# Attention's own rows by block load instead of gather, and VectorE's steps of two interleaved streams held in written order

## The chip, the cores and the metric

The kernel is one program on one core of a Trainium2 chip. Its time is device microseconds, the median of three runs. TensorE (PE) multiplies, VectorE (DVE) and ScalarE (ACT) do elementwise work and reductions, GpSimd (POOL) here mostly writes the descriptors of indirect DMAs (gathers and scatters by a list of row numbers), and SyncE (SP) issues plain DMAs. Each engine works through its own instruction queue in order and waits at an instruction until its inputs are there.

## The reference

Four graph layers run one after another on x, 8 batches of 2048 nodes with 64 features, each of the form x = x + layer(relu(layernorm(x))). The change lies where the third layer (index 2) ends and in the fourth (index 3). Cut to these:

```python
# third layer, three steps; its last step gives v, and x = x + v
effects = einsum('nm,bmd->bnd', adj, v)
v = relu(concat([v, effects]) @ W1.T + b1) @ W2.T + b2
# fourth layer: attention over all 2048 nodes
h = x @ weight                       # 8 batches x 64 = 512 numbers a node
e = leaky_relu((h @ a[:64])[:, :, None] + (h @ a[64:])[:, None, :], 0.2)
e = adj * e                          # adj holds 0 and 1: no edge gives e = 0, not minus infinity
out = softmax(e) @ h + bias
```

Since a missing edge counts with exp(0 - top) and not with zero, the kernel takes the sum of h over all nodes once (`total`), scaled by exp(-top), and corrects it for the few neighbours that each node has.

## The kernel before, in words

**The fourth layer's tiles.** Nodes are ranked by degree; the 16 tiles of 128 nodes are tiles of ranks, not of node numbers. `order` holds, for tile t, the 128 node numbers of its ranks (`order[:, 1, t]`, the gather list) and, the other way round, the ranks of the 128 nodes of node tile t (`order[:, 0, t]`). Tile 0, the nodes of highest degree, is done densely (`Near.first_tile`). Tiles 1 to 15 are done from lists of neighbours (`Near.others`), in the order `TILES = [15, 13, 11, 1, 10, 2, 9, 3, 8, 4, 7, 5, 6, 12, 14]`.

**What a tile needs.** In the third layer's last step `Scores.chunk` makes h for every node tile (512 numbers a node, kept in SBUF as `rows(t)`) and 16 scores a node, and SP writes both to a DRAM table `f_rows` (528 numbers a row, L2899 and L2900). `Near.block(t)` then fills n = NEAR[t] + 1 places of a ring of 36 with indirect DMAs from `f_rows` that POOL issues (L2966): place 0 is the tile's own rows, by `order`, the others its neighbours, by `near`. The first two blocks are asked for ahead of everything, and block `place + 2` at the end of the tile at `place`.

**A sparse tile's work** (L2998 to L3052). The opening: L3011 adds the tile's own score to the neighbours' scores (it reads all n places, so it waits for all of them), then L3015 to L3028 are small DVE and ACT steps that make the weights `e`, `none` and `den`. The body: DVE multiplies rows by weights into `y` (L3056 for one row, L3037 for two; y has four places), and PE adds each of the n + 1 results to `acc` in PSUM by a product with the identity matrix. The close: DVE writes `o` = `acc` x `den` (L3056), and one tile later POOL scatters `o` to `att_rows` (L2977).

**The dense tile's work** (`first_tile`, L3061 to L3146). It gathers 128 rows of adj (L3067) and its own rows `mine`, makes scores, and then takes 16 steps, one for each source tile jt: 16 exponentials on ACT (L3119, L3120), `tensor_max` (L3123) and `tensor_mul` (L3124) on DVE, and 8 products of 128x65 and one of 128x512 (`plain`) on PE. Its `m` has two buffers for each of two terms, so the exponentials of step jt wait for the products of step jt - 2.

**How the two are woven.** Both are generators. `layer3_near` (L2067) takes the first piece of each, then 12 more pieces of `first_tile` (up to and with the `tensor_mul` of jt = 2), then one piece of `first_tile` after each piece of `others`. This is the written order. It isn't the issue order: a planner ahead of the run sorts each engine's instructions by its own estimates of when inputs will be there, keeping what the data need. `kern.behind(x)` (L193) ties x, in issue order alone, behind the instruction written just before it on the same engine. It is used before in `Lists.fill`, and nowhere in the fourth layer.

**The third layer's end.** In its last step the same weaving has `Feed` gather rows `raw` for PE (L2636, POOL), while `advance` takes pieces of `chunk` for groups of 4, 4, 4, 2 and 2 node tiles (L2864 to L2901). `order` is a tile of this layer, written by `neighbours` and stored to DRAM (`order3`); the fourth layer loads it back.

**The end.** After all scatters SP loads `att_rows` back (L3152), PE transposes it, DVE adds x, and ACT issues the stores (L3148 to L3167).

Of the kernel before, what the change touches and what calls it, by code (L numbers as in the profile page):

```python
# [7 lines left out]
F = mybir.dt.float32  # L8
# [3 lines left out]
I32 = mybir.dt.int32  # L12
AF = mybir.ActivationFunctionType
OP = mybir.AluOpType
# [5 lines left out]
P = 128  # L20
NB = 8
N = 2048
D = 64
# [112 lines left out]
class Kernel:  # L136
# [8 lines left out]
    def __init__(self, tc, ctx, a):  # L145
        self.tc, self.nc, self.a = tc, tc.nc, a
        self.flip = 0
        self.short = False
        self.consts = ctx.enter_context(tc.tile_pool(reuse_waits="tile", name="consts", bufs=1))

        dram = ctx.enter_context(tc.tile_pool(reuse_waits="tile", name="dram", bufs=1, space=bass.MemoryType.DRAM))
        self.xs = [
            [a["xT"][:, :, c * CW : (c + 1) * CW].rearrange("q p n -> p q n") for c in range(NC)]
        ]


        self.h_rows = dram.tile([N, ROW], F, name="h_rows")
        self.g_rows = dram.tile([N, NB * D], F, name="g_rows")
        self.order3 = dram.tile([P, 2, NT], I32, name="order3")

        self.links = dram.tile([N, N], BF, name="links")
        self.sent = [dram.tile([N, NB * D], F, name=f"sent{i}") for i in range(5)]


        self.f_rows = dram.tile([N, WIDE], F, name="f_rows")
        self.att_rows = dram.tile([N, NB * D], F, name="att_rows")
        self.rdeg = dram.tile([NT, P], F, name="rdeg")

        self.h_sums = [dram.tile([8, P, CW], F, name=f"sums{q}") for q in range(NP)]
        self.h_parts = [dram.tile([P, 3, N], BF, name=f"parts{q}") for q in range(NP)]  # L170
        for i in range(3):
            self.xs.append([dram.tile([P, NP, CW], F, name=f"x{i}_{c}") for c in range(NC)])
        self.setup()
# [1841 lines left out]
    def neighbours(self, k, bank, slots):  # L2015

        nc = self.nc
        order = k.tile([P, 2, NT], I32, name="order")  # L2020
        w = Parts(slots.tile([P, 2 * N], F, name="sort", tag="q4"))
        rank = self.ranks(w, bank, 1, NEAR[1])
        yield
        self.by_rank(w, bank, rank, order)
        nc.sync.dma_start(self.order3, order)
        yield
        near = self.near
        words = slots.tile([P, 2, N], F, name="near_rows", tag="q4")
        rows = words[:, 0].bitcast(BF).rearrange("p (i n) -> p i n", i=2)
        named = words[:, 1].bitcast(F16).rearrange("p (i n) -> p i n", i=2)  # L2030
        words = slots.tile([P, 2, N], F, name="line", tag="q5")
        whole = words[:, 0].bitcast(I32)
        line = words[:, 1, : N // 2].bitcast(F16)
        nc.gpsimd.iota(whole, pattern=[[1, N]], base=1, channel_multiplier=0)
        nc.vector.tensor_copy(line, whole)
        yield
        for t in range(1, NT):
            raw, row = rows[:, t % 2], named[:, t % 2]
            nc.gpsimd.indirect_dma_start(
                raw, None, self.links[:],  # L2040
                bass.IndirectOffsetOnAxis(ap=order[:, 1, t : t + 1], axis=0),
            )
            nc.vector.tensor_mul(row, raw, line)
            yield
            most = -(-NEAR[t] // 8)
            top = k.tile([P, 24], F, name="top", bufs=2)
            for i in range(most):
                eight = top[:, 8 * i : 8 * i + 8]
                nc.vector.max(out=eight, in_=row)
                yield  # L2050
                if i + 1 < most:
                    nc.vector.match_replace(
                        out=row, in_to_replace=eight, in_values=row, imm_value=0.0
                    )
                    yield
            nc.vector.tensor_copy(near[:, FIRST[t] : FIRST[t + 1]], top[:, : NEAR[t]])
# [521 lines left out]
class Feed:  # L2578
# [82 lines left out]
    def own(self, t):  # L2661
        if t < HUBS:
            return None
        own = self.w.tile([P, CW], F, name="own", bufs=min(2, self.AHEAD))
        self.nc.sync.dma_start(own, self.rows[t * P : (t + 1) * P])
        return own
# [166 lines left out]
class Scores:  # L2833
# [30 lines left out]
    def chunk(self, col, first, n):  # L2864
        nc, kern = self.nc, self.kern
        here = slice(first % TC * P, (first % TC + n) * P)
        x, xr, sq, hn = (a[:, :, here] for a in (self.x, self.xr, self.sq, self.hn))

        def write(q, _, xr, scale):
            nc.vector.scalar_tensor_tensor(  # L2870
                hn[:, q], xr, 1.0, scale, op0=OP.mult, op1=OP.mult,
                accum_out=self.sums[:, q, col : col + 1],
            )

        if here.start == 0:
            self.std = self.w.tile([P, CW], F, name="std", bufs=1)
        std = self.std[:, here]
        yield from kern.norm_parts(
            None, x, xr, sq, std, lambda: self.bank()[:, : n * P], write,
            heat=8 if n < TC else 0,  # L2880
        )
        yield
        for t in range(first, first + n):
            i = t % TC
            scores = kern.scores[:, t].rearrange("n (i q s) -> n q i s", i=2, s=2)
            for g in range(2):
                pn = self.ps.tile([P, 2, 256], F, name="pw", tag="pn")
                for j in range(2):
                    kern.mm(
                        pn[:, j, : P + 4], self.hn[:, 2 * g + j, i * P : (i + 1) * P], self.wide  # L2890
                    )
                to = self.rows(t)[:, 2 * g * P : 2 * (g + 1) * P]
                kern.copy(to.rearrange("n (j c) -> n j c", j=2), pn[:, :, :P])
                nc.vector.tensor_copy(
                    scores[:, 2 * g : 2 * g + 2],
                    pn[:, :, P : P + 4].rearrange("n q (i s) -> n q i s", i=2),
                )
            to = kern.f_rows[t * P : (t + 1) * P]
            nc.sync.dma_start(to[:, : NB * D], self.rows(t))  # L2899
            nc.sync.dma_start(to[:, NB * D :], kern.scores[:, t])  # L2900
            yield  # L2901

    def end(self):
        nc = self.nc
# [11 lines left out]
class Near:  # L2916
# [48 lines left out]
    def fetch(self, to, index):  # L2965
        self.nc.gpsimd.indirect_dma_start(  # L2966
            to, None, self.kern.f_rows[:], bass.IndirectOffsetOnAxis(ap=index, axis=0)
        )

    def leave(self, t, o):  # L2970

        self.back.append((t, o))
# [9 lines left out]
    def block(self, t):  # L2982

        n = NEAR[t] + 1
        if self.at + n > self.RING:
            self.at = 0
        here = range(self.at, self.at + n)
        assert not set(here) & set(self.unread)
        self.unread = here
        block = self.ring[:, self.at : self.at + n]  # L2990
        self.at += n
        self.fetch(block[:, 0], self.order[:, 1, t : t + 1])
        for i in range(n - 1):
            c = FIRST[t] + i
            self.fetch(block[:, 1 + i], self.near[:, c : c + 1])
        return block

    def others(self):  # L2998
# [3 lines left out]
        for place, t in enumerate(self.TILES):  # L3002
# [5 lines left out]
            top = w.tile([P, NB], F, name="top", bufs=2)  # L3008
            none = w.tile([P, NB], F, name="none", bufs=2)
            den = w.tile([P, NB], F, name="den", bufs=2)  # L3010
            nc.vector.tensor_tensor(  # L3011
                e, block[:, :, NB * D : NB * D + NB], es.unsqueeze(1).to_broadcast(full),
                op=OP.add,
            )
            nc.vector.scalar_tensor_tensor(e, e, 0.2, e, op0=OP.mult, op1=OP.max)  # L3015
            there = self.there[:, FIRST[t] : FIRST[t + 1]].unsqueeze(2)
# [44 lines left out]
    def first_tile(self):  # L3061
# [21 lines left out]
            nc.scalar.copy(at[:, 4 * g : 4 * g + 4], pt)  # L3083
        yield
        mine = w.tile([P, WIDE], F, name="mine")
        self.fetch(mine, self.order[:, 1, :1])

        es = mine[:, NB * D + NB :]
        top = w.tile([P, NB], F, name="first_top")
# [24 lines left out]
        for jt in range(NT):  # L3114
            h = hs[jt % 2]
            nc.scalar.copy(h[:, :, :D], self.rows(jt).rearrange("n (b f) -> n b f", b=NB))
            m, m2 = (self.m[:, 2 * (jt % 2) + i] for i in range(2))
            for b in range(NB):
                nc.scalar.activation(m[:, b], on_all[:, 0, b], AF.Exp, bias=ed[:, jt, b : b + 1])  # L3119
                nc.scalar.activation(m2[:, b], on_all[:, 1, b], AF.Exp, bias=ed2[:, jt, b : b + 1])  # L3120
                if b % 4 == 3:
                    yield
            nc.vector.tensor_max(m, m, m2)  # L3123
            nc.vector.tensor_mul(m, m, at[:, jt].unsqueeze(1).to_broadcast([P, NB, P]))  # L3124
            yield
            kern.mm(plain, at[:, jt], self.rows(jt), start=jt == 0, stop=jt == NT - 1)
            for b in range(NB):
                kern.mm(
                    accs[b // 4][:, b % 4, : D + 1], m[:, b], h[:, b],
                    start=jt == 0 and b % 4 == 0, stop=jt == NT - 1 and b % 4 == 3,  # L3130
                )
            yield
# [144 lines left out]
```

## Time and profile before

| | |
|---|---|
| median of 3 runs | 1938.78 us (1930.53 to 1944.4) |
| profiled execution's own time | 1938.07 us |
| its span, first to last instruction | 1936.3 us |
| mean granted TensorE clock | 0.933 |
| busy, share of the span | PE 88%, DVE 73%, POOL 54%, ACT 42% |
| last `f_rows` write issued | 1654.6 us into the span |
| first gather of the fourth layer | 1660.27 us |
| close of the last sparse tile (`o` of tile 14) | 1899.95 to 1900.64 us |
| span's end | 1936.3 us |

The page puts 1.8 us around the span. Times in lines of a timeline are microseconds from the span's start; in the lines of groups the two numbers behind the first bar are the total busy time in microseconds and the mean of one in nanoseconds, and behind the second bar stands how long the engine sat idle just before them, with what ended it. "issue" there is time in which the engine waited for nothing that the profile shows. A PE product of 32-bit numbers shows as two instructions.

### The profile page before, as it was taken

The numbers are of one execution on the slowest core, as the hardware profiler recorded it, in microseconds if no ns is written. First come the engines' busy times: TensorE is split into PE (matmuls) and PEld (weight loads), VectorE is DVE, ScalarE is ACT, GpSimd is POOL, SyncE is SP. The second block draws the span as 40 slices with busy tenths as digits, with TensorE's granted clock in tenths as the row PEclk, the third lists the DMA queues.
The fourth block names the chain that finished last, engine by engine and source line by source line (L and its number), as shares of the span: only waits on it lengthen the run. The fifth ranks groups of instructions, "written<-read, shape, count | busy, mean of one in ns | idle before, by whom it ended". The sixth has DMA issues, their size and how long they took to land. (4 is left out here: it accounts for less than half of the span.)

```text
span 1936.3 us, 22507 instructions
## 1 busy us (share of the span) xinstructions
PE 1695.0 (88%) x7139; PEld 972.7 (50%) x7139; DVE 1407.0 (73%) x2312; ACT 818.9 (42%) x1650; POOL 1048.6 (54%) x1007
## 2 busy tenths in 40 slices
PE   6888999998997788999999999689799899679885
PEld 2445766664334544443443444467577576345432
DVE  6888788874667688776776656788888576458874
ACT  5732544454656644222111100366666654356300
POOL 1101466677753646876656456276474641577770
PEclk8898999998987898999999989879989999789887
DMA  9741223335535864242230210478788774766665
GB/s 342 278 122 46 76 88 109 104 116 186 173 111 166 240 193 151 71 108 83 59 110 28 88 42 24 167 233 269 227 266 269 218 243 157 233 178 175 183 173 199
DMA packets 127226, 305.22 MB, mean 158 GB/s; under 512 B 29536, under 2 KB 33392, under 8 KB 121968
## 3 DMA queue, kind: packets, MB, share of 16 engines
q0 software_dynamic: 45328, 149.60, 26.2%
q1 hardware_dynamic: 79456, 149.81, 23.3%
q10 hardware_dynamic: 2304, 4.20, 0.6%
q8 instruction: 60, 0.98, 0.2%
q14 instruction: 78, 0.64, 0.1%
HBM read 240.40 MB, written 63.14 MB: 157 GB/s over the span
## 5 line engine op out<-in xcount | busy, mean ns | idle before, releaser
L2636 POOL DMA_INDIRECT raw<-sent,index x300 | 320.0, 1067 | 277.0 <-DVE part_lo L2654 114.9
L2653 ACT CAST part_hi<-raw 128x512 fp32r<-128x512 f32 x352 | 213.8, 619 | 325.6 <-PE acc L177 212.5
L2654 DVE TENSOR_TENSOR part_lo<-raw,part_hi 128x512 fp32r<-128x512 f32 x352 | 266.1, 780 | 92.3 <-ACT part_hi L2653 82.6
L177 PE MATMUL pk<-q,w 128*128 128x512 f32 (+1 forms) x768 | 303.3, 608 | 2.0 <-DVE q L1750 0.9
L1863 POOL TENSOR_TENSOR half<-half,y 128x512 f32<-128x512 f32 x180 | 230.3, 1308 | 120.2 <-DVE y L1856 119.6
L177 PE MATMUL acc<-q,ident 128*128 128x512 f32 x416 | 202.8, 613 | 23.1 <-DVE q L3056 17.0
L177 PE MATMUL acc<-part_lo,weights 128*128 128x512 f32 x365 | 167.0, 459 | 34.2 <-DVE part_lo L2654 33.7
L177 PE MATMUL acc<-part_hi,weights 128*128 128x512 f32 x365 | 173.6, 479 | 22.2 <-ACT part_hi L2653 21.7
L177 PEld LDWEIGHTS pk<-q,w 128*128 128x128 f32 (+1 forms) x768 | 115.5, 189 | 152.4 <-issue 117.4
L1856 DVE SCALAR_TENSOR_TENSOR y<-pk,bias,q 128x512 f32<-128x512 f32 x210 | 148.1, 744 | 54.9 <-PE pk L177 36.7
L2966 POOL DMA_INDIRECT ring<-f_rows,near x121 | 141.7, 1171 | 64.6 <-issue 29.2
L177 PEld LDWEIGHTS acc<-q,ident 128*128 128x128 f32 x416 | 77.0, 194 | 96.8 <-issue 42.9
L177 PEld LDWEIGHTS acc<-part_lo,weights 128*128 128x128 f32 x365 | 73.1, 200 | 87.9 <-DVE part_lo L2654 74.2
L2345 POOL TENSOR_TENSOR q<-q,beta 128x512 f32<-128x512 f32 x57 | 76.0, 1335 | 71.3 <-DVE beta L2321 32.6
L177 PEld LDWEIGHTS acc<-part_hi,weights 128*128 128x128 f32 x365 | 72.8, 199 | 71.4 <-ACT part_hi L2653 39.6
L177 PE MATMUL pp<-adj,x_ind_hi 128*128 128x512 f32 x256 | 89.5, 465 | 0.5 <-DVE q L882 0.3
L300 DVE RECIPROCAL std<-std 128x512 f32<-128x512 f32 (+1 forms) x17 | 53.8, 3162 | 32.6 <-ACT std L299 32.6
L3037 DVE TENSOR_TENSOR q<-ring,e 128x1024 f32<-128x1024 f32 x58 | 70.1, 1220 | 9.0 <-PE acc L177 8.8
L2622 ACT CAST hub_weights<-dense 128x384 fp32r<-128x384 uint8 x80 | 40.5, 511 | 84.1 <-PE acc L177 83.6
L2345 POOL TENSOR_TENSOR q<-q,coef 128x512 f32<-128x512 f32 x57 | 63.0, 1106 | 21.0 <-DVE q L2368 17.6
L2553 POOL DMA_INDIRECT listed_raw<-in_adjT_dram,cell x60 | 63.8, 1063 | 16.5 <-issue 16.1
L177 PE MATMUL pp<-adj,x_ind_lo 128*128 128x512 f32 x256 | 72.7, 403 | 0.0
(510 smaller groups left out, 3482.3 us busy)
## 6 DMA issues: line engine op xcount, KB each, us to landing
rows<-in_adj_dram SPq DMA_DIRECT2D x16, 1024.0 KB, 8.9
adj_t<-in_adjT_dram SPq DMA_DIRECT2D x64, 256.0 KB, 3.0
own<-sent SPq DMA_DIRECT2D x52, 256.0 KB, 4.1
raw<-sent SPq DMA_DIRECT2D x52, 256.0 KB, 3.5
sent<-u SPq DMA_DIRECT2D x48, 256.0 KB, 4.0
q<-x SPq DMA_DIRECT2D x9, 1024.0 KB, 5.0
links<-squares POOLq DMA_DIRECT2D x16, 512.0 KB, 8.0
sent<-q SPq DMA_DIRECT2D x32, 256.0 KB, 3.6
```

What stands on the lines that cost most here:

```text
L177: self.nc.tensor.matmul(out, lhsT, rhs, start=start, stop=stop)
L300: nc.vector.reciprocal(std, std)
L1856: nc.vector.scalar_tensor_tensor(y, pks[b, half], bias[:, b : b + 1], emb[:, b], op0=OP.add, op1=OP.mult,)
L1863: add.tensor_add(acc, acc, y)
L2345: self.nc.gpsimd.tensor_tensor(x, x, by.unsqueeze(2).to_broadcast([P, NB, D]), op=OP.mult)
L2553: self.kern.behind(nc.gpsimd.indirect_dma_start(raw[:, i], None, rows, bass.IndirectOffsetOnAxis(ap=self.cell[:, c + i : c + i + 1], axis= ...
L2622: self.nc.scalar.copy(to, self.lists.dense[:, :, i * P : (i + 1) * P])
L2636: self.nc.gpsimd.indirect_dma_start(raw, None, self.rows[:], bass.IndirectOffsetOnAxis(ap=self.lists.index[:, c : c + 1], axis=0),)
L2653: nc.scalar.copy(hi, raw)
L2654: nc.vector.tensor_sub(lo, raw, hi.bitcast(F))
L2966: self.nc.gpsimd.indirect_dma_start(to, None, self.kern.f_rows[:], bass.IndirectOffsetOnAxis(ap=index, axis=0))
L3037: nc.vector.tensor_tensor(y.rearrange("n i (b f) -> n i b f", b=NB), block[:, i : i + 2, : NB * D].rearrange("n i (b f) -> n i b f", b=NB) ...
```

## The change

It has two parts.

1. Two new DRAM tables, `own_h` and `own_scores`, hold the rows in rank order. When a node tile's `f_rows` are written, POOL also scatters its rows and scores there, by `order[:, 0, t]`, which is kept as `kern.nodes`: 32 indirect DMAs in `Scores.chunk`. In the fourth layer place 0 of each block, and `mine`, are then loaded by SP with two plain DMAs each (32 in all) in place of 16 indirect ones by POOL.
2. Two DVE instructions of the fourth layer are tied by `behind`: each tile's opening sum (L3011) and each dense step's `tensor_max` (L3123).

```diff
+        self.own_h = dram.tile([N, NB * D], F, name="own_h")
+        self.own_scores = dram.tile([N, 2 * NB], F, name="own_scores")
...
-        order = k.tile([P, 2, NT], I32, name="order")
+        order = self.nodes = k.tile([P, 2, NT], I32, name="order")
...
             nc.sync.dma_start(to[:, NB * D :], kern.scores[:, t])
             yield
+            at = bass.IndirectOffsetOnAxis(ap=kern.nodes[:, 0, t : t + 1], axis=0)
+            nc.gpsimd.indirect_dma_start(kern.own_h[:], at, self.rows(t), None)
+            nc.gpsimd.indirect_dma_start(kern.own_scores[:], at, kern.scores[:, t], None)
...
+    def own(self, to, t):
+
+        dma, rows = self.nc.sync.dma_start, slice(t * P, (t + 1) * P)
+        dma(to[:, : NB * D], self.kern.own_h[rows])
+        dma(to[:, NB * D :], self.kern.own_scores[rows])
+
...
-        self.fetch(block[:, 0], self.order[:, 1, t : t + 1])
+        self.own(block[:, 0], t)
...
-            nc.vector.tensor_tensor(
-                e, block[:, :, NB * D : NB * D + NB], es.unsqueeze(1).to_broadcast(full),
-                op=OP.add,
+            kern.behind(
+                nc.vector.tensor_tensor(
+                    e, block[:, :, NB * D : NB * D + NB], es.unsqueeze(1).to_broadcast(full),
+                    op=OP.add,
+                )
             )
...
-        self.fetch(mine, self.order[:, 1, :1])
+        self.own(mine, 0)
...
-            nc.vector.tensor_max(m, m, m2)
+            kern.behind(nc.vector.tensor_max(m, m, m2))
```

## The prediction

> **What bounds the kernel now.** I read the page first, then the busy table by stage, then groups, waits and each engine's timeline of the fourth layer. That layer runs from 1655 to the close of tile 14 at 1900.6; what follows (scatter, reload, transposes, stores, 36 us) is untouched. In it POOL is the bound. From the groups of 1655 to 1937 us:
>
> ```profile
> L2966 POOL DMA_INDIRECT ring<-f_rows,near x121 | 141.7, 1171 | 64.6 <-issue 29.2 <-DVE own L3072 24.6 <-DVE den L3027 3.8
> L2966 POOL DMA_INDIRECT ring<-f_rows,order x15 | 15.5, 1032 | 4.6 <-issue 4.0 <-DVE den L3026 0.3 <-DVE q L3037 0.3
> L2977 POOL DMA_INDIRECT att_rows<-o,order x15 | 20.0, 1331 | 15.5 <-DVE o L3056 6.8 <-DVE top L3019 2.8 <-DVE q L3037 2.5
> ```
>
> Apart from the 24.6 us ahead of the first gather, POOL's idle time is the 0.30 us between two instructions, one wait of 3.8 us, and waits for the last `o`. Its timeline confirms it: 1660.27 to 1882.58 without a real hole but one.
>
> ```profile
> 1660.27 0.94 POOL L2966 DMA_INDIRECT ring<-f_rows,near  x1 [24.59 <-DVE own L3072]
> ...
> 1729.79 1.76 POOL L2966 DMA_INDIRECT ring<-f_rows,near  x1 [3.79 <-DVE den L3027]
> ...
> 1881.64 0.94 POOL L2966 DMA_INDIRECT ring<-f_rows,near  x1 [0.30 <-issue]
> ```
>
> DVE in turn stalls at openings that are issued before their gathers have landed, 38 us in all. The list of waits:
>
> ```profile
> DVE e L3011 <- DMA att_rows<-o,order: 15.1, 1, 15.1
> DVE e L3011 <- DMA ring<-f_rows,near: 14.3, 3, 9.4
> ...
> DVE e L3011 <- DMA ring<-f_rows,order: 8.5, 1, 8.5
> ```
>
> But the same early issue also hides things. In DVE's timeline tile 15 opens at 1672, 28 us before dense step 2 is ready for DVE (1700.69), and the opening of tile 14 (128x40) stands ahead of the close of the tile before it, while PE still adds that one up:
>
> ```profile
> 1672.17 0.19 DVE L3011 TENSOR_TENSOR e<-ring 128x32 f32<-128x32 f32 x1
> ...
> 1673.55 0.69 DVE L3056 TENSOR_TENSOR q<-q,none 128x512 f32<-128x512 f32 x1
> ...
> 1675.11 0.69 DVE L3056 TENSOR_TENSOR q<-ring,e 128x512 f32<-128x512 f32 x1
> ...
> 1700.69 1.23 DVE L3123 TENSOR_TENSOR q<-q 128x1024 f32<-128x1024 f32 x1 [2.82 <-ACT q L3120]
> ...
> 1886.11 0.20 DVE L3011 TENSOR_TENSOR e<-ring 128x40 f32<-128x40 f32 x1
> ...
> 1887.87 0.68 DVE L3056 TENSOR_TENSOR o<-acc,den 128x512 f32<-128x512 f32 x1
> ```
>
> **Part 1, own rows: what it removes.** 15 gathers of 1.03 us and `mine` of 0.95, each with its 0.30: 15 x 1.33 + 1.25 = 21.2 us of POOL's queue. If POOL stayed the bound, tile 14 would close at 1879.4.
>
> **What it adds in the third layer.** 32 scatters. The nearest row is the scatter of `o`, 1.33 + 0.30 = 1.63 us: 52 us of POOL. Half of them, for node tiles 0 to 7, come between 1557 and 1600 beside the raw gathers, which take 33 us of POOL from 1551 to 1605 in the busy table (24.8 busy, and 26 x 0.30 between them); free are 54 - 33 = 21 us, wanted are 16 x 1.63 = 26. A scatter also waits in POOL's queue for the copies of `rows(t)`, and the raw gathers behind it feed PE, which is busy throughout there (49.8 of 50 us). Bounds: -3 (a luckier plan; nothing is removed in this stage) and +12 (two batches, each putting the gathers off by some 6 us past what the six raw buffers cover). I take +4. The other 16 meet an idle POOL. The last four start when tile 14's copies are done, 1652.7, and need 4 x 1.63: POOL is free at 1659.2, and the first gather can't start before the order list, 1659.5. SP's own loads wait for all scatters to land, some 3 us later, and behind a waiting own load on SP stand only other own loads, x and the reload at 1903; they have 30 us before anyone needs them. Hand-over: 0, at most +3.
>
> The Trainium skill speaks against the small scatter: "DMA: Bandwidth & Descriptors", Specifications, gives 512 B as the least transfer at full rate, below which the DMA engine reads, changes and writes; `own_scores` goes in pieces of 64 B. The write of the same scores to `f_rows` landed in 1.9 us against 2.2 for the 256 KB beside it, so no row shows such a cost, and by it only a landing that has 30 us to spare would be later.
>
> **Part 2, written order: the start.** The instruction written on DVE just before tile 15's opening is the `tensor_mul` of dense step 2, since 12 pieces of `first_tile` are written first. So tile 15 can't open before three dense steps are through ACT and DVE. `ex` was made at 1681.3; without the work of tiles 15 and 13 before it I put it at 1679. Then PE and four copies 3.3, 48 exponentials at the 0.295 us between two starts 14.2, the wait of step 2 for the products of step 0 1.1, max and mul 2.3: 1699.9. I take 1699 (1696 to 1703) in place of 1672.2. POOL doesn't mind at first: it fills the ring until about 1705.
>
> **Part 2: each tile's border.** The instruction written just before an opening is the close of the tile before it, and that waits for PE's last product. So nothing of the next tile is ready on DVE when PE runs out. From the row of tile 15: close 0.2 + 0.6, opening to the end of the first `y` 1672.17 to 1674.24 = 2.07: PE idle 2.9. Its product takes 0.89, the second `y` is ready at +3.63 from the opening (0.6 more idle), the first pair at +4.84 (0.3 more). Together 3.8 a border, against 0.3 in the tail of before. 14 borders: 53 us.
>
> **The new chain on PE**, from tile 15's opening:
> - first `y`: 1699 + 2.1 = 1701
> - 151 products into `acc` (136 ring rows + 15 totals) at 1.77 / 2 = 0.885 (chain of waits, four instructions): 134
> - 13 dense steps' products of 1.67 (1.06 + 0.61 in the chain): 22; `plain`, 17.5 us, stands mostly in PE's idle time before 1699: 4
> - 14 borders: 53; last close 0.7
>
> 1701 + 134 + 22 + 4 + 53 + 0.7 = 1914.7, 14 us later than 1900.6, and 35 later than POOL alone would allow: POOL's 21 us are won and not seen, since PE and DVE have become the bound.
>
> **PE's clock at the borders.** After 8.42 us idle four instructions took 3.78 us, after none 1.94, so a cold restart costs 1.84; after 1.24 us idle (1870.58) there was no loss:
>
> ```profile
> 1798.55 3.78 PE L177 MATMUL acc<-q,ident 128*128 128x512 f32 x4 [8.42 <-DVE q L3056]
> ...
> 1870.58 9.71 PE L177 MATMUL acc<-q,ident 128*128 128x512 f32 x22 [1.24 <-DVE q L3037]
> ```
>
> Bounds for 14 borders of 2.9 us: 0 and 14 x 1.84 = 26. 2.9 is nearer to 1.24, so I take two restarts, +4.
>
> The Trainium skill, "TensorE: Matmul & The Clock Gate", Part 1: The HAM clock gate, has the array fall to half rate after an idle window of about 3.4 us, counted by a free-running clock. A border of 2.9 us with 0.6 behind it lies just at that; taken at its word a few borders would pay, which agrees with the choice above.
>
> **Sum.** 14 + 4 (clock) + 4 (third layer) = +22 on the profiled execution's 1938.07, which lies 0.7 under the median: **1960**.
>
> **The rivals.**
> - *Cover (18%).* All dense products stand in the borders and no restart is cold: 1914.7 - 22 = 1893, +4: 1934. For it: PE ran dense products between the sparse ones all through before. Against: a dense step's max and mul are written ahead of the close, so its products are mostly ready before the border.
> - *POOL stays the bound (14%), the other side.* The place is POOL's queue, the price -21.2, +4 in the third layer: 1921. It decides if the PE chain above falls under 1879, that is if borders and start together cost 35 us less than I say. For it: 38 us of DVE stalls at early openings go, and `mine` comes sooner. Against: those stalls fell where POOL was the bound, so they cost nothing by themselves.
> - *Cold at every border (12%).* 1914.7 + 26 + 4: 1983; the third layer's +12 would come on top of any case.
>
> My own case has 56%, and 1945 to 1976 as its range (start -3 to +4, third layer -3 to +12, clock 0 to +12); about 70% of it lies over 1957.5. A per cent, 19 us, is about what a measurement of this kernel can tell from no change: its three runs lie 14 us apart. Slower by over 1%: 0.56 x 0.7 + 0.12 = 0.51. Within: 0.56 x 0.3 + 0.17 = 0.34. Faster: 0.15, POOL's case and a little of the cover's. The range 1925 to 1986 leaves out most of POOL's case and the worst sums.
>
> **What would show it.** Tile 15's L3011 near 1699; every later L3011 right behind an `o`; PE idle some 3 us at each of 14 first `y`s; no DVE wait for gathers at L3011 worth naming; POOL with real holes in the fourth layer (waits for ring places read by DVE), its gathers fewer by 16; `o` of tile 14 near 1915 to 1922. Wrong would be: L3011 of tile 15 well before 1696, openings whose softmax runs while PE still has products, POOL without holes, or PE holes near 1560 to 1600 over 12 us.

## The result, and the profile after

The changed kernel takes **1985.1 us** (1971.99 to 1987.93), the kernel before 1938.78: a ratio of **1.0238** with a 95% interval of 1.0204 to 1.0272, 46 us slower. That lies at the very end of the whole range given (1925 to 1986) and past the range of the prediction's own case (1945 to 1976), and the forecast, +22, has under half of the move.

The profiled execution of the changed kernel took 1971.99 us, 13 under its median. The profiled executions of all kernels here reach the first `f_rows` write of scores, the first place that the change can touch, between 1548.6 and 1563.1 us, whatever the kernel; this one at 1548.6, that of before at 1558.0. So stretches are compared from that write on. From it to the span's end before takes 378.3 us and after 421.6: +43.3, which answers to the +46 of the medians.

| stretch, us (profiled execution) | before | after | difference | forecast |
|---|---|---|---|---|
| third layer's end: first to last `f_rows` write of scores | 96.6 | 109.1 | +12.5 | +4 |
| hand-over: last such write to the first gather into the ring | 5.7 | 8.65 | +3.0 | 0, at most +3 |
| first gather to the opening of tile 15 | 11.9 | 46.0 | +34.1 | +26.8 |
| opening of tile 15 to the close of tile 14 | 227.8 | 221.1 | -6.7 | -8.8 |
| close of tile 14 to the end | 36.35 | 36.7 | +0.3 | 0 |

The forecast of the fourth row is (1914.7 - 0.7) - 1699 + 4 for the clock = 219 against 227.8, that of the third 1699 - 1660.27 = 38.7 against 11.9.

**The start.** VectorE's timeline of after (start, duration, engine and line; in brackets the idle time before, and what ended it):

```profile
1682.34 2.35 DVE L3087 SCALAR_TENSOR_TENSOR q<-q,own 128x2048 f32<-128x2048 int32 x1 [13.95 <-DMA q<-in_adj_dram,order]
...
1700.09 1.23 DVE L3136 TENSOR_TENSOR q<-q 128x1024 f32<-128x1024 f32 x1 [8.34 <-ACT q L3133]
...
1710.00 1.23 DVE L3136 TENSOR_TENSOR q<-q 128x1024 f32<-128x1024 f32 x1 [0.43 <-ACT q L3133]
1711.26 1.23 DVE L3137 TENSOR_TENSOR q<-q,q 128x1024 f32<-128x1024 f32 x1
1712.40 0.18 DVE L3023 TENSOR_TENSOR e<-ring 128x32 f32<-128x32 f32 x1
...
1721.84 0.69 DVE L3069 TENSOR_TENSOR o<-acc,den 128x512 f32<-128x512 f32 x1 [2.99 <-PE acc L179]
1722.44 0.19 DVE L3023 TENSOR_TENSOR e<-ring 128x40 f32<-128x40 f32 x1
```

Tile 15's sum (L3023, L3011 before) starts right behind the multiplication of dense step 2 (L3137), as forecast, with no idle time ahead of it. Tile 13's stands right behind tile 15's `o`. What is late is the first line: the dense tile's adjacency rows arrive 15.9 us after the first gather (1666.40), where before they came after 9.3 (1669.59 - 1660.27).

**The borders.** TensorE's timeline of after, four of the last first products of a tile:

```profile
1886.07 11.22 PE L179 MATMUL acc<-q,ident 128*128 128x512 f32 x22 [3.25 <-DVE e L3038]
...
1900.45 11.70 PE L179 MATMUL acc<-q,ident 128*128 128x512 f32 x20 [3.16 <-DVE e L3038]
...
1915.27 8.01 PE L179 MATMUL acc<-q,ident 128*128 128x512 f32 x14 [3.12 <-DVE e L3038]
...
1926.41 7.08 PE L179 MATMUL acc<-q,ident 128*128 128x512 f32 x12 [3.12 <-DVE e L3038]
```

Each begins after some 3.1 us in which TensorE has nothing, since the softmax of the opening (L3038 is in it) is only now being made. In this trace the idle time ahead of the first product is 36.7 us at the 14 borders together, 2.6 each: 3.0 to 3.6 us at eight of them, and 1.2 to 2.2 at the six where the products of a dense step stood in the border. The groups of 1658 to 1970 us (busy us, mean ns of one; behind the second bar the idle time before them and what ended it):

```profile
L179 PE MATMUL acc<-q,ident 128*128 128x512 f32 x302 | 156.4, 669 | 38.1 <-DVE e L3038 24.4 <-DVE q L3069 12.3 <-DVE q L3050 1.0
L2971 POOL DMA_INDIRECT ring<-f_rows,near x121 | 147.7, 1220 | 49.6 <-issue 27.1 <-DVE den L3040 6.9 <-DVE den L3041 3.6
...
L2988 POOL DMA_INDIRECT att_rows<-o,order x15 | 17.6, 1171 | 52.0 <-DVE e L3023 36.9 <-DVE o L3069 9.2 <-issue 4.6
...
L3069 DVE TENSOR_TENSOR o<-acc,den 128x512 f32<-128x512 f32 x15 | 10.4, 691 | 28.0 <-PE acc L179 28.0
```

The same group of products before (1655 to 1937 us):

```profile
L177 PE MATMUL acc<-q,ident 128*128 128x512 f32 x302 | 144.2, 620 | 20.6 <-DVE q L3056 17.0 <-DVE q L3037 3.5
```

The 15 gathers by `order` are gone. POOL, which had one real hole before, now sits idle 52 us ahead of its scatters of `o` (15.5 before), most of it in waits that a border's end released (L3023). VectorE in turn waits 28.0 us at the closes for TensorE, 3.9 before. The list of waits has no wait of L3023 for a gather any more. So TensorE and VectorE, one after the other, have become the bound, not POOL.

**The third layer's end.** Busy time by stage, before and then after (length, then PE, PEld, DVE, ACT, POOL, with the number of instructions; granted clock, DMA share, GB/s; PEld is TensorE's loading of weights):

```profile
1550.00:1600.00 50.00, 49.80 (x260) 35.46 (x260) 36.53 (x78) 29.83 (x63) 21.77 (x22) 1.00 0.77 245
1550.00:1600.00 50.00, 40.09 (x193) 27.19 (x193) 28.08 (x56) 22.70 (x48) 24.73 (x26) 0.93 0.66 212
```

TensorE was busy 49.8 of these 50 us before and is now 40.1. POOL's timeline there and the list of waits from 1540 to 1662 (us in total, times, longest) show what it waits for:

```profile
1559.16 1.00 POOL L2905 DMA_INDIRECT own_h<-q,order  x1 [0.90 <-DMA own_h<-q,order]
1560.46 1.00 POOL L2906 DMA_INDIRECT own_scores<-scores,order  x1 [0.30 <-issue]
1561.77 0.98 POOL L2638 DMA_INDIRECT raw<-sent,index  x1 [0.30 <-issue]
1564.48 0.98 POOL L2905 DMA_INDIRECT own_h<-q,order  x1 [1.73 <-DMA own_h<-q,order]
```

```profile
ACT part_hi L2655 <- DMA raw<-sent,index: 17.1, 7, 5.1
...
PE bank L179 <- DVE q L296: 8.6, 3, 7.7
```

Eight pairs of scatters stand among the raw gathers, and four of them wait, in POOL's queue, until one of the pair before has landed (0.57 to 1.73 us, 4.0 in all). The gathers `raw` stand behind them: reckoned from the first `f_rows` write, the ninth of the last 25 goes out 9.4 us later than before, and the last 20.0 us later. ScalarE waits for them 17.1 us, its squares for the norm come late, and TensorE stops once for 7.7 us.

At the hand-over the last two pairs wait in the same way. POOL's timeline of after:

```profile
1657.32 0.97 POOL L2905 DMA_INDIRECT own_h<-q,order  x1 [1.38 <-DVE q L193]
1661.71 0.97 POOL L2906 DMA_INDIRECT own_scores<-scores,order  x1 [3.42 <-DMA own_scores<-scores,order]
1663.86 0.97 POOL L2905 DMA_INDIRECT own_h<-q,order  x1 [1.18 <-DMA own_scores<-scores,order]
1665.13 0.97 POOL L2906 DMA_INDIRECT own_scores<-scores,order  x1 [0.30 <-issue]
1666.40 1.00 POOL L2971 DMA_INDIRECT ring<-f_rows,near  x1 [0.30 <-issue]
```

### The profile page after: what moved, and what is told of

Read it like the earlier page. It is cut to its first block, busy times and chain, and to the rows that moved or that the text cites. A ratio compares the mean times of both kernels' runs of the same rounds, so it can differ in the third digit from the quotient of the medians.

```text
span 1970.2 us, 22642 instructions
## 1 busy us (share of the span) xinstructions
PE 1705.7 (87%) x7139; PEld 969.0 (49%) x7139; DVE 1414.2 (72%) x2312; ACT 818.8 (42%) x1650; POOL 1060.1 (54%) x1023
## 5 line engine op out<-in xcount | busy, mean ns | idle before, releaser
L179 PE MATMUL acc<-q,ident 128*128 128x512 f32 x416 | 215.1, 649 | 40.6 <-DVE e L3038 24.4
L2971 POOL DMA_INDIRECT ring<-f_rows,near x121 | 147.7, 1220 | 49.6 <-issue 27.1
L179 PEld LDWEIGHTS acc<-q,ident 128*128 128x128 f32 x416 | 81.3, 205 | 132.0 <-issue 85.7
```

The costliest lines, as they stand in the source:

```text
L179: self.nc.tensor.matmul(out, lhsT, rhs, start=start, stop=stop)
L2971: self.nc.gpsimd.indirect_dma_start(to, None, self.kern.f_rows[:], bass.IndirectOffsetOnAxis(ap=index, axis=0))
```

## The experiments

The first table has every kernel's time and its ratio to the kernel before, run on the same chip; kernels of different chips are compared by these ratios. The second has its stretches, named as in the table above.

| kernel | median, us | ratio | 95% interval |
|---|---|---|---|
| the change | 1985.1 | 1.0238 | 1.0204 to 1.0272 |
| 1 own rows alone | 1940.86 | 1.002 | 0.9998 to 1.0042 |
| 2 written order alone | 1962.37 | 1.0135 | 1.009 to 1.018 |
| 3 scatters alone | 1947.11 | 1.0068 | 1.0035 to 1.01 |
| 4 change, maxima not tied | 1989.15 | 1.0268 | 1.0224 to 1.0312 |
| 5 own rows, scatters late | 1944.13 | 1.0014 | 0.9995 to 1.0034 |
| 6 change, first opening free | 1979.75 | 1.0207 | 1.0185 to 1.0229 |
| 7 change, borders filled | 1980.24 | 1.0217 | 1.0178 to 1.0257 |
| 8 as 5, with early tied openings | 1934.8 | 0.9978 | 0.9948 to 1.0008 |
| 9 change, start spread | 1971.94 | 1.0155 | 1.012 to 1.019 |
| 10 before, with early tied openings | 1932.27 | 0.9972 | 0.995 to 0.9993 |

| profiled execution, us | third layer's end | hand-over | to the opening of 15 | from it to the close of 14 | first gather to close |
|---|---|---|---|---|---|
| before | 96.6 | 5.7 | 11.9 | 227.8 | 239.7 |
| after | 109.1 | 8.65 | 46.0 | 221.1 | 267.1 |
| 1 | 109.1 | 6.35 | 10.7 | 220.5 | 231.2 |
| 2 | 96.5 | 3.4 | 39.65 | 225.0 | 264.6 |
| 3 | 107.8 | 11.85 | 12.7 | 220.5 | 233.2 |
| 4 | 107.5 | 9.0 | 45.5 | 228.4 | 273.9 |
| 5 | 95.2 | 17.8 | 11.4 | 222.8 | 234.2 |
| 6 | 109.5 | 8.3 | 10.0 | 254.2 | 264.2 |
| 7 | 111.25 | 5.8 | 46.8 | 215.0 | 261.8 |
| 8 | 96.6 | 17.2 | 10.6 | 212.9 | 223.5 |
| 9 | 107.7 | 9.2 | 9.7 | 246.0 | 255.7 |
| 10 | 96.55 | 5.7 | 12.0 | 226.1 | 238.1 |

The theory was that of the prediction: the openings tied behind the closes, and the first behind dense step 2, cost the most, the scatters the rest. The rivals: the tied maxima, the loads of own rows, a cold TensorE.

### 1 to 3: one part alone

Kernel 1 leaves out both ties, kernel 2 both tables with their scatters and loads. Kernel 3 adds the scatters to the kernel before, and nobody reads them:

```diff
 # kernel 1, against the changed kernel
-            kern.behind(nc.vector.tensor_tensor(e, block[...], es..., op=OP.add))
+            nc.vector.tensor_tensor(e, block[...], es..., op=OP.add)
-            kern.behind(nc.vector.tensor_max(m, m, m2))
+            nc.vector.tensor_max(m, m, m2)
 # kernel 3, against the changed kernel, beside the same
-        self.own(block[:, 0], t)
+        self.fetch(block[:, 0], self.order[:, 1, t : t + 1])
```

> The change's first part alone: own rows scattered and loaded as blocks, nothing tied on VectorE. Theory A (the written order alone makes the loss; the own rows shorten POOL's queue): POOL stays the bound of the fourth layer, 16 gathers fewer are worth 21 us, the scatters cost 4 to 8 at the third layer's end: 1921 to 1927. Theory B (the scatters make a good part of the loss, since each waits for the one before to land, and the first gather comes 6 us later): 1940 or more. First gather of the fourth layer near 1666 by both.

> The change's second part alone: openings and dense maxima tied, gathers as before. Theory A: tile 15's opening only after dense step 2, near 1701, some 12 us sooner than with both parts since the third layer ends as before, and then the same chain of PE and borders of 222 us: last close near 1924, time 1960 to 1975. Theory B: the order is close to free, 1938 to 1945.

> The 32 scatters to the new tables, which nobody reads: gathers as before, nothing tied. It prices the scatters by themselves. Theory A: the first gather of the fourth layer comes 6 us later and the time is 1938 + 6, up to 1946. Theory B: 1955 or more.

Own rows alone come out level (1.002), the order alone costs 1.35%, 26 us. In the second table the two parts touch different stretches. The third layer's end is 108 to 109 us wherever the scatters stand where the change puts them (1, 3, the change), and 96.5 without. The start is 40 or 46 us wherever the ties stand, and 11 to 13 without.

The parts don't add up. The change's ratio is +46 us, and those of kernels 1 and 2 together are 4 + 26 = 30. From the second table: against kernel 2 the change has +12.6 in the third layer, +5.2 in the hand-over, +6.3 in the start, and only -3.9 in the rest. Own rows alone shorten the stretch from first gather to close by 8.5 us against before (kernel 1), and of this nothing is left where the ties have made TensorE and VectorE the bound. Kernel 3 warns against reading this stretch as POOL's queue alone: it has all the gathers and is 6.5 us shorter than before too, with a hand-over that is 6.2 longer. Counted from the last write to the close, kernel 1 has 7.5 us less than kernel 3, which has the same scatters.

### 4: which of the two ties

```diff
-            kern.behind(nc.vector.tensor_max(m, m, m2))
+            nc.vector.tensor_max(m, m, m2)
```

> Both parts, but the dense maxima not tied, only the openings. Theory A: the borders stay and so does the start (tile 15's opening stays behind the multiplication of dense step 2); only the spread of dense steps may be better: within 10 us of the whole change, 1970 to 1990. A rival, theory C (the tied maxima are what hurts, since they can no longer be drawn into idle time of VectorE): 1940 to 1955.

No gain: 1.0268 against 1.0238, with intervals that overlap, and the start is the same 45.5 us. The tied maxima aren't what costs.

### 5: the scatters behind the gathers

Part 1 alone again, but the scatters are kept back until the third layer's last `raw` gather is written, and the first is tied behind it on POOL:

```diff
-            nc.gpsimd.indirect_dma_start(kern.own_h[:], at, self.rows(t), None)
-            nc.gpsimd.indirect_dma_start(kern.own_scores[:], at, kern.scores[:, t], None)
+            self.pending.append(t)       # issued after the last raw gather,
+            if self.released:            # the first two by kern.behind(...)
+                self.scatter()
```

> The first part alone, as in the first experiment, but the scatters of the node tiles whose rows are ready early are put behind the last raw gather on POOL's queue (tied to it), and the others follow as before. If scatters between raw gathers cost the 12 us that the stretch from the first to the last write of f_rows grew by in all four kernels with scatters (96.6 to 108 and 109), that stretch is back at 97 and the time falls from 1941 to 1928 to 1936. If it is the mere number of POOL instructions and bytes, wherever they stand, it stays at 1938 to 1944.

That settles where the third layer's term comes from: the scatters' place among the raw gathers. Busy time by stage of kernel 5:

```profile
1550.00:1600.00 50.00, 49.81 (x263) 35.45 (x264) 37.97 (x76) 29.84 (x62) 20.78 (x21) 1.00 0.77 247
```

TensorE is full again, and the end of the layer is back at 95.2 us. But the time stays (1.0014), since the chain of scatters is now last. POOL's timeline of kernel 5 around the hand-over:

```profile
1668.05 0.97 POOL L2915 DMA_INDIRECT own_h<-q,order  x1 [1.27 <-DMA own_scores<-scores,order]
1669.32 0.97 POOL L2918 DMA_INDIRECT own_scores<-scores,order  x1 [0.30 <-issue]
1671.54 0.97 POOL L2915 DMA_INDIRECT own_h<-q,order  x1 [1.25 <-DMA own_scores<-scores,order]
1672.82 0.97 POOL L2918 DMA_INDIRECT own_scores<-scores,order  x1 [0.30 <-issue]
1674.09 0.99 POOL L2986 DMA_INDIRECT ring<-f_rows,near  x1 [0.31 <-issue]
```

A pair takes 3.5 us, where the prediction's row gave 2 x 1.63 = 3.3: the instructions are shorter, 0.97, but each pair here waits until one of the pair before has landed, though POOL has nothing else to do. The last pairs end at 1674, and the hand-over goes from 6.35 to 17.8 us.

### 6: the first opening free

```diff
-            kern.behind(nc.vector.tensor_tensor(e, block[...], es..., op=OP.add))
+            opened = nc.vector.tensor_tensor(e, block[...], es..., op=OP.add)
+            if place:
+                kern.behind(opened)
```

> The whole change, but the opening of tile 15, the first of the sparse tiles, isn't tied; all others are. Theory A has the start priced at some 28 us: tile 15 opens within 20 us of the first gather, not 46 behind it, and tiles 15, 13 and 11 are through while the first dense steps are being made; tile 1 then waits for its last gather, near 1718. Time 1957 to 1965 in place of 1985. If the start was hidden by the gathers anyway: 1975 or more.

The opening comes 10.0 us after the first gather, as meant, and yet the time falls by no more than some 6 us by the ratios, within the two intervals. TensorE's timeline of kernel 6:

```profile
1681.81 2.07 PE L179 MATMUL acc<-q,ident 128*128 128x512 f32 x2 [20.88 <-DVE q L3069]
1688.08 1.97 PE L3095 MATMUL pt<-ident,q 128*128 128x128 f32 x8 [4.20 <-DVE q L3087]
1689.84 1.91 PE L179 MATMUL acc<-q,ident 128*128 128x512 f32 x2
...
1701.01 1.02 PE L179 MATMUL acc<-q,ident 128*128 128x512 f32 x2
1701.87 5.31 PE L179 MATMUL plain<-q,q 128*128 128x512 f32 x12
```

Tile 15's five products are spread from 1681.8 to 1702.0, between transposes of the adjacency rows (`pt`, L3095) and `plain`. Its close comes at 1702.07, and the tied opening of tile 13 at 1702.68, where dense steps 0 to 2 (maxima at 1704.5, 1709.2, 1714.4) stand around it. So the start's price isn't that of one opening. It is the order of the whole first stretch.

### 7: the borders filled

At every border TensorE gets 13 products of identity by zeros into a bank of its own, behind the tile's last product:

```diff
+            some = kern.ident[:, : P // 2].bitcast(BF)
+            for _ in range(13):
+                kern.behind(nc.tensor.matmul(
+                    heat, some, kern.zeros.to_broadcast([P, CW]), start=True, stop=True
+                ))
```

> The whole change, and at each tile's border 13 products of the identity with zeros into a spare bank, tied behind the tile's last product on PE, 2.8 us at full clock: PE isn't idle while VectorE closes one tile and opens the next. Nothing that is computed changes. If the array falls to its slow clock at the borders (products into acc took 669 ns on average against 620 before, 302 of them: 15 us), the time falls from 1985 to 1968 to 1975. If only the idle time counts, 1983 to 1990.

The groups of kernel 7 from 1658 to 1970 us:

```profile
L179 PE MATMUL acc<-q,ident 128*128 128x512 f32 x302 | 144.0, 618 | 5.5 <-DVE e L3039 2.1 <-DVE q L3051 1.7 <-DVE q L3075 0.9
...
L3064 PE MATMUL heat<-cols,ident 128*128 128x512 bf16 x184 | 43.0, 379 | 0.6
```

The idle time before `acc` products falls from 38.1 to 5.5 us, and one takes 618 ns, as before the change (620), and not 669: 144.0 us in all and not 156.4. The granted clock goes with it. The 22 instructions that took 11.22 us in the change (1886.07) had a clock of 0.86, and the same 22 take 10.19 us in kernel 7 at 1.00. Yet from the opening of tile 15 to the last close it takes 215.0 us against 221.1, and the ratio, 1.0217, can't be told from 1.0238. So the lower clock costs 12.4 us on these products, and it isn't the main cost of the change. That only 6.1 us come back is in part due to the filling itself. At the last five borders the tile's first product starts 3.1 to 3.3 us after the last one of the tile before, just as in the change, but at five earlier ones it comes right behind the filling products, 0.4 to 1.4 us later than in the change.

### 8 and 10: openings written one part early

Kernel 8 is kernel 5 with both ties, but each opening except the first is written ahead of the previous tile's last part, and tied there, not behind its close. Kernel 10 does that alone to the kernel before: gathers for own rows, no tables, free maxima.

```diff
             for i in range(-1, n, 2):
+                if i + 2 >= n and ready:
+                    opened = self.opening(self.TILES[place + 1], ready[0], True)
                 y = self.y[:, self.turn % 4 : self.turn % 4 + 2]
```

> Own rows with late scatters, and the written order itself changed: a tile's opening is written ahead of the last part of the tile before it (and tied there, as the dense maxima are), and tile 15's isn't tied. If the borders and the start are what the tied order costs, PE has products while the next tile opens, POOL is the bound again with 16 gathers fewer: 1915 to 1930. If tied openings cost for another reason (VectorE waiting for gathers), 1945 or more.

> The kernel before with one edit: each sparse tile's opening, but the first, is written one part before the end of the tile ahead of it and tied there. No own tables, no scatters, own rows by gather as before, dense maxima free. If the borders' idle TensorE is what a tied opening costs, and the early openings of before that stall VectorE on gathers (38 us in all) cost something as well, the stretch from the first gather to the last sparse close is 225 to 235 us against 239.7 before, the end of the third layer stays at 96 to 97 us and the hand-over at 3 to 6: 5 to 15 us faster than before (1925 to 1935). If the 121 gathers, with own rows 137, bound the layer at this place anyway (1660 to 1882 without a hole), the time is that of before within 4 us.

Kernel 8 takes the border's price off: from first gather to close 223.5 us, against 264.2 in kernel 6, which differs by this and by the scatters' place (worth +3.0 in this stretch, kernel 5 against 1). That is 40.7 us, 2.9 for each of 14 borders, or 3.1 if the 3.0 are added. It isn't idle time alone: in the groups the products on `acc` are busy 145.3 us in kernel 8 and 161.5 in kernel 6, and tile 13, which no longer waits for tile 15's close, opens 21.6 us after the first gather and not 33.0. All TensorE waits of over 2 us in kernel 8 from 1690 to 1905:

```profile
1695.18 1.97 PE L3117 MATMUL pt<-ident,q 128*128 128x128 f32 x8 [3.52 <-DVE q L3109]
...
1862.52 15.80 PE L179 MATMUL acc<-q,ident 128*128 128x512 f32 x30 [2.20 <-DVE q L3072]
```

Only the second is one at a sparse product. In kernel 10 the same edit is worth next to nothing in this stretch, 238.1 against 239.7, though 5 to 15 was hoped for. POOL's groups of kernel 10:

```profile
L2966 POOL DMA_INDIRECT ring<-f_rows,near x121 | 147.8, 1221 | 61.1 <-issue 30.2 <-DVE own L3081 24.6 <-DMA ring<-f_rows,near 2.7
...
L2966 POOL DMA_INDIRECT ring<-f_rows,order x15 | 14.7, 980 | 4.6 <-issue 3.7 <-DMA att_rows<-mine,order 0.3 <-DVE top L3016 0.3
```

POOL issues from 1654.13 to 1876.69 without a hole of 2 us: by this it is the bound, with 222.6 us from its first gather to its last. That length isn't fixed, though: kernel 3 issues the same gathers without a hole in 212.4 us. Own rows, once the borders don't take POOL's place, are worth at most 238.1 - 223.5 = 14.6 us of the 21.2 in the queue (kernel 8 has tied maxima, which kernel 4 shows to matter little). How much of the 14.6 is only kernel 8's later first gather, as in kernel 3, is not shown. Kernel 8 gives back 17.2 - 5.7 = 11.5 of it at the hand-over, so that 3.1 are left from the last write to the close, and it ends level with before. Kernel 10 is the only one whose interval lies below 1, by 0.28% (0.07% to 0.5%).

### 9: the dense steps not ahead

```diff
-            for _ in range(12):
-                next(first)
+            next(first)
...
-            for part in others:
+            for place, part in enumerate(others):
                 next(first, None)
+                if place < 11:
+                    next(first, None)
```

The first opening is free as in kernel 6.

> The whole change, with two differences in the written order alone: only one piece of the dense tile is written ahead of the sparse tiles instead of thirteen, and each of the first eleven parts of the sparse tiles is followed by two dense pieces instead of one; and the first sparse tile's opening isn't tied. So dense steps 0 to 2 no longer stand, tied, ahead of tiles 15 and 13. If the late start is what costs (46 us from the first gather to the opening of tile 15, and the openings of 13 and 11 behind dense step 2), tile 15 opens some 10 to 12 us after the first gather, tile 13 well before 1700, and the stretch from the first gather to the last sparse close falls from 267 us to 242 to 255: 12 to 25 us less than the whole change, the dense steps' 8 us on TensorE now standing among the sparse products. If the start is hidden, because TensorE waits for the adjacency row until about 1696 in either order, the stretch stays at 262 to 267 us, as when the first opening alone was freed (264).

The stretch falls to 255.7 us, just above the upper end of what the start's theory gave, and the time by 13 us (1.0155; 16 by the ratios). VectorE's timeline of kernel 9:

```profile
1689.28 0.19 DVE L3023 TENSOR_TENSOR e<-ring 128x32 f32<-128x32 f32 x1 [7.73 <-DMA ring<-f_rows,near]
...
1707.86 0.19 DVE L3023 TENSOR_TENSOR e<-ring 128x40 f32<-128x40 f32 x1
...
1715.02 1.22 DVE L3137 TENSOR_TENSOR q<-q 128x1024 f32<-128x1024 f32 x1 [5.65 <-ACT q L3134]
```

Tile 13 opens 28.3 us after the first gather (56.0 in the change), but still waits for tile 15's close, whose products stand around the late transposes. Against kernel 6 the three dense steps written ahead cost 8.5 us of the stretch; the rest goes with the ties at the borders and, as far as these lines tell, with the late adjacency rows.

## Why the prediction was right or wrong

The direction was right, and so were the places where the time goes. Three terms were too small, all of them from part 1 or from where the two parts meet: the third layer by 8.5 us, the hand-over by 3.0 and the start by 7.3. They make 18.8 of the 21 us between the +22 of the forecast and the +43.3 of the two traces. The prediction's own case allowed the start +4 and the third layer +12, so both went past their upper ends.

- **"I take +4" for the scatters in the third layer** failed: 12.5 us, just past its own upper bound of 12. The working weighed POOL's free time, 21 us, against 26 wanted. The instructions were even shorter, 0.97 us and not 1.33, so that the eight pairs would nearly have fitted, and yet the time was lost: what counts is how long the raw gathers behind a batch are put off. They were 9.4 us late after the first four pairs and 20.0 at the end, where the upper bound had two times 6. The working also left out that a scatter waits for an earlier one to land, 4.0 us of POOL's time there. Kernel 5 shows the place to be the cause: scatters out of that stretch, and the 12.5 us are gone. How they divide between the scatters' own instructions and the waits for landings, no run shows.
- **"Hand-over: 0, at most +3"** came out at its bound, 3.0. The last four scatters, two pairs, were priced as 4 x 1.63 = 6.5 us of POOL. They take 8.8, from 1657.32 to 1666.10, with waits of 3.42 and 1.18 us for landings among them. The prediction let only the loads on SP, with 30 us to spare, wait for landings. But the next scatters on POOL wait too, and the first gather behind them.
- **"I take 1699" for tile 15's opening**: the cause was right (behind step 2's multiplication, 21.1 us from `ex` at 1691.33 to 1712.40, forecast 20 from 1679 to 1699). For part 2 alone the whole term was right too: 39.65 us after the first gather in kernel 2, forecast 38.7. In the change it is 46.0. "I put it at 1679" for `ex` is the step that failed. It held the adjacency rows to come as before, but their gather went fourth into POOL's queue (1670.22, 3.8 us after the first) and not second (1661.52, 1.25 after), and VectorE had them 12.1 us after the issue, not 8.1. The place in the queue comes with the scatters and the longer landing with the loads of own rows: kernel 3, with the scatters and without the loads, has the gather fourth too, but its rows after 6.6 us, and every kernel with the loads after 11.5 to 12.5. That the loads take the DMA engines' time from the gather is a likely reason, not one that a run isolated.
- **The chain on TensorE** was right in sum, 219 against 221.1, by luck, since two sizes offset each other. The borders were put at 53 us, and TensorE's idle time before `acc` products is 38.1 in all (20.6 before), 36.7 of it at the borders. The products on `acc` were put at 134 us and the clock at two cold restarts, +4, together 138; they are busy 156.4 (144.2 before). The clock's part is 12 of this, at the upper end of the range: kernel 7 takes it away and is back at 144.0. At 3.25 us of idle time 22 instructions took 11.22 us, against 9.71 behind 1.24 us in the row that the prediction showed. So 2.9 was nearer to the cold end than to the warm one.
- **"POOL's 21 us are won and not seen"** was right: the last gather is issued at 1885.62, the last close comes at 1933.53. Kernels 8 and 10 put what is won at 14.6 us at most where POOL stays the bound, kernels 1 and 3 at 7.5 with the order as it was.
- The rivals: *cover* falls, the dense products shorten six of the 14 borders and fill none. *POOL stays the bound* holds only without the ties, and even then (kernel 1) the scatters take it back. *Cold at every border* gave a time near the one measured, 1983, in part by luck: its +26 for the clock is 12 in the traces, and its +4 for the third layer 12.5. Kernel 7 takes the cold products away and hardly any time is won.

The Trainium skill, "TensorE: Matmul & The Clock Gate", Part 1: The HAM clock gate, puts the idle window at about 3.4 us; here a border of 3.25 us by the profile already cost 1.0 us (against kernel 7) to 1.5 us (against before) in its products, at a granted clock of 0.86, so the measured row decides, and a border of some 3 us isn't to be counted as warm. "DMA: Bandwidth & Descriptors", Specifications, has transfers below 512 B as not at full rate, and no row here shows a price for it: the scatter of 64 B pieces landed in a median of 3.4 us and that of 2 KB pieces in 3.1 in the change, but in 2.4 and 3.9 in kernel 5. The list of DMA issues of after from 1540 to 1668 us (median us to landing):

```profile
own_h<-q,order POOLq DMA_INDIRECT x16, 3.1
own_scores<-scores,order POOLq DMA_INDIRECT x16, 3.4
```

## What to carry to other kernels

An instruction tied behind a close takes over the close's wait, so price what the next engine has to do meanwhile, and what the idle time does to its clock; writing the opening one part earlier kept the order and gave back some 3 us a border, of idle time and clock together. Before adding instructions to a queue, ask what stands behind them and how late it may be, not only whether the engine has free time. A run of indirect writes can be paced by their landings, as here, 3.5 us a pair, and whatever stands behind them in that engine's queue waits too. Work taken off the engine that bounds is worth its queue time only as far as the next engine's chain is shorter: here 21 us of queue were 14.6 at most, 7.5 with the order as it was, and none with the ties.

## What the runs showed that was not expected

- The instruction of a scatter into the new tables takes 0.97 us, less than the 1.33 of the scatters of `o`. The wait for a landing adds 0.7 to 3.1 us where there is one in kernel 5, and the sixteen pairs take 66.6 us there (1607.2 to 1673.8), other waits among them.
- At one border of only 1.97 us (1778.48 in the change) the clock was down as well, 0.85, and 16 instructions took 8.90 us; at another, of 2.22 us (1791.34), it was 1.00, and 16 took 7.84.
- Freeing one opening by 36 us (kernel 6) moved the time by no more than 6, because TensorE takes its products in order and some of them wait for rows that come late in any case.
